# A fixed TensorE order for the mixer, MLP and routing of a Mamba2 and mixture-of-experts layer

## The chip, the cores and the metric

The kernel runs on one core of one Trainium2 chip. The metric is the device time of one execution in microseconds (us). The core has five engines that run side by side[...]: TensorE (PE; its weight loads are the row PEld), VectorE (DVE), ScalarE (ACT), GpSimd (POOL) and SyncE (SP), which here only issues DMAs. TensorE writes to PSUM[...]; the other engines read the results from there.

## The reference, cut to what matters

Input: 2048 tokens of width 512, float32. `A` is a layer of its own with an inner residual; the matrices are all float32.

```python
x = x + A(layernorm(x))                  # A: mixer, then MLP
x = x + E(layernorm(x))                  # E: experts

def A(u):
    h = u + mamba2(rmsnorm(u))
    h2 = rmsnorm(h)
    return h + (silu(h2 @ gate_w) * (h2 @ up_w)) @ down_w       # 512 -> 2048 -> 512

def mamba2(v):
    z, xb, B, C, dt = split(v @ in_proj_w)    # 1024, 256, 256, 1024, 16 columns
    xb, B, C = silu(causal_conv4(xb, B, C))
    dt = softplus(dt + dt_bias); dA = dt * -exp(A_log)          # 16 heads of 64
    # chunks of 128 tokens; L[q, s] = exp(cum[q] - cum[s]) for s <= q, cum = cumsum(dA)
    y = (C @ B.T * L) @ (xb * dt) + exp(cum) * (C @ state)
    state = state * exp(cum[-1]) + (B * exp(cum[-1] - cum)).T @ (xb * dt)
    y = rmsnorm((y + D * xb) * silu(z)) @ out_proj_w
    return y

def E(v):
    p = softmax(v @ Wr)                       # 8 experts, the 2 best, weights made to sum to 1
    return sum(w_e * (silu(v @ Wg[e]) * (v @ Wu[e])) @ Wd[e] for e in top2(p))  # 512 -> 352 -> 512
```

## The kernel before

**Tiles.** A chunk is 128 tokens (`P`), a token block two chunks (`TB` = 256, index `b`, 8 of them), an MLP block two token blocks (`FB` = 512, index `fb`, 4 of them).

**The mixer.** `prepare(b)` normalizes a block, transposes it into `hT` (L186), makes the step sizes dt and dA with some 20 small VectorE operations, and their sums `pc` (L246), `pn` and `psum`. The rows of sums go to HBM, and `spread` reads them back spread over partitions as `cum` and `ec`; GpSimd masks `cum` (L282). `project` makes one of six column pairs `pm` of the convolved part (16 matmuls, L301), ScalarE copies it to `pre` (L311), VectorE does the four taps (L318, L320), ScalarE the SiLU (L326). GpSimd keeps the three tokens that the next block needs in `halo`. `gate` makes the four pairs `pz` of silu(z). `chunk` is the core: transposes `ptx`, scores `psc` (L363), decays on ScalarE (L369), their product with the scores on VectorE (`cum`, L371, eight instructions for each half of the heads), `py` from the old state (L384) and from this chunk (L390), the new state `pst` (L397, L413), skip and gate (`yd` L403, `zs` L406), squares (L422 to L425, the sums on GpSimd), output projection `po` (L430), sum of squares `pms` (L432), its root `ry` (L142), the residual `h`, and a transposition of the normalized `h2` (L448) for the MLP.

**The MLP.** `feed_forward(fb)` runs 16 steps c over 128 columns of the hidden width each. The gate and up products of a step are made as a two by two block product with seven block multiplications instead of eight (`product`, L644: two matmuls of 256 columns each). Sums of the weights are made by GpSimd in the first pass (`load_early`, `load_late`), written to HBM on ScalarE's DMA queue and read in the later passes; sums of the activations come from `sums`. Two PSUM banks carry a step: `px` (tag x1) is written and read five times one after the other, `py` (tag x2) twice. Its readers are ScalarE copies (L665, L667, L675) and VectorE (L671, L679, L680, L685). `mlp_down` adds the previous two steps' contribution to the output for 128 tokens: two matmuls of 512 columns into `pd` (L629) and one VectorE addition into `r` (L630).

**Routing and experts.** `route(fb, rows)` normalizes the finished rows, transposes them (`xT`, copied by ScalarE, L188), makes the logits (L542), picks the two best with small VectorE operations, counts places, and builds lists of tokens with one-hot products `pls` (L606). `table` turns counts and lists into at most 39 tiles of 128 tokens. `tiles` then gathers each tile by an indirect DMA (L865), multiplies it with its expert's weights (L884, L896, L905), and adds it to the output by an indirect DMA (L911). The first eight tiles use the lists of the first three MLP blocks alone.

**What sets the order.** The stages are Python generators that are stepped against each other, and this is the source's order:

```python
for _ in mamba(b):          # one piece per yield of a chunk: three or four in each
    if feed:
        next(feed)          # one MLP step of the block before
    if tail:
        next(tail, None)    # one piece of the routing of the block before that
```

That order isn't the engines'. The Tile framework's planner gives each engine its own order by planned costs and due times, so that it may bring a matmul group forward or put it back. Instructions of one engine then run in the order given.

**PSUM.** Eight banks: `ps_x` two (`px`, `py`), `ps_mm` three under one tag (`pd`, `po`, `pm`, `pz`, and all transposes and small products), `ps_sg` two (`psc`), `ps_y` one (`py` of the chunk).

**The opening.** SP issues the loads of x, `params`, `w_dt`, two pairs of `w_in` (`wi`), then `w_o` (2 MB), then the router's weights. GpSimd scales `w_o` in eight instructions before it comes to the halo copies of the first block. `prepare(0)` runs to its end, `spread` follows, and then the six projections of block 0.

Of the kernel before, what the change touches and what calls it, by code (L numbers as in the profile page):

```python
# [49 lines left out]
def mamba_mlp_moe(ctx, tc, x, w_in, w_out, w_gu, w_down, par, wr, wg, wu, wd, out):  # L50
# [47 lines left out]
    nc.sync.dma_start(out=w_o, in_=w_out.rearrange("(t p) n -> p t n", p=P))  # L98
# [64 lines left out]
    ps_mm = psa_stack.enter_context(tc.tile_pool(name="ps_mm", bufs=3, space=PSUM))  # L163
# [3 lines left out]
    use = {"g": (ps_x, "x1"), "u": (ps_x, "x2"), "d": (ps_mm, "mm"), "tr": (ps_mm, "mm")}  # L167
# [24 lines left out]
    def prepare(b):  # L192

        scales(b)
        hT = wa.tile([P, NK, TB], F32, name=f"hT{b}", tag="hT")
        for j in range(NCH):
            t = b * NCH + j
            hn = wa.tile([P, D], F32, name=f"hn{t}", tag="tok", bufs=3)
            nc.vector.tensor_scalar(
                hn, res[t], mv[:, t, 0:1], rboth[:, t : t + 1], ALU.subtract, ALU.mult  # L200
            )
            transposed(hn, hT[:, :, j * P : (j + 1) * P], params[:, C_L1 : C_L1 + NK])
# [6 lines left out]
        pdt = ps_mm.tile([P, NCH, NH], F32, name=f"pdt{b}", tag="mm")  # L209
# [35 lines left out]
        pc = ps_mm.tile([P, P], F32, name=f"pc{b}", tag="mm")  # L245
# [5 lines left out]
        nc.sync.dma_start(out=rows_d.rearrange("a n q -> n a q"), in_=rows)  # L251

        pn = ps_mm.tile([P, NCH, NH], F32, name=f"pn{b}", tag="mm")
# [7 lines left out]
        psum = ps_mm.tile([P, 2, NCH, NH], F32, name=f"psum{b}", tag="mm")  # L261
# [32 lines left out]

    def projected(b, pair, pm, hT):
        w = ahead.pop(0)
        if b < NB - 1 or pair < 8:
            ahead.append(load_w_in((pair + 2) % 10))
        for m in range(2):
            for k in range(NK):  # L300
                nc.tensor.matmul(  # L301
                    pm[:, m, :], w[:, k, m * P : (m + 1) * P], hT[:, k, :], start=(k == 0), stop=(k == NK - 1)
                )

    def project(b, pair, hT, xb, cs):

        pm = ps_mm.tile([P, 2, TB], F32, name=f"pm{b}_{pair}", tag="mm")
        projected(b, pair, pm, hT)
# [19 lines left out]
    def gate(b, pair, hT, zs):  # L328

        pm = ps_mm.tile([P, 2, TB], F32, name=f"pz{b}_{pair}", tag="mm")  # L330
        projected(b, 6 + pair, pm, hT)
        nc.scalar.activation(zs[:, 2 * pair : 2 * pair + 2, :], pm, AF.Silu)
# [7 lines left out]

    def chunk(b, j, dt, ncum, dtdec, cd, cum, ec, xb, cs, zs):
        t = b * NCH + j
        tok = slice(j * P, (j + 1) * P)
        halves = [slice(half * HD, (half + 1) * HD) for half in range(2)]
        sdt = sdiag[t % 2]
        y = zs[:, :, tok]


        pt = ps_mm.tile([P, 4, P], F32, name=f"ptx{t}", tag="mm")
        for m in range(4):  # L350
            nc.tensor.transpose(pt[:, m, :], xb[:, m, tok], ident)
        xbt = wa.tile([P, 2, 4, HD], F32, name=f"xbt{t}", tag="xbt")
        nc.scalar.copy(xbt.rearrange("p a g d -> p (a g d)"), pt.rearrange("p a q -> p (a q)"))

        for gp in range(2):
# [18 lines left out]
            if gp == 0 and t < NT - 1:  # L374
# [5 lines left out]
                )  # L380
            py = ps_y.tile([P, 4, P], F32, name=f"py{t}_{gp}", tag="y")
# [6 lines left out]
            yield  # L388
            for half in range(2):
# [4 lines left out]
            if gp == 0 and t < NT - 1:  # L394
                pst = ps_mm.tile([P, 2, 4, HD], F32, name=f"pst{t}", tag="mm")
# [23 lines left out]


# [10 lines left out]
        pms = ps_mm.tile([P, 1], F32, name=f"pms{t}", tag="mm")  # L431
# [8 lines left out]
        nc.scalar.dma_start(out=resd[t], in_=res[t])  # L440
        yield
# [12 lines left out]

    for m in range(8):
        nc.gpsimd.tensor_scalar_mul(w_o[:, m, :], w_o[:, m, :], params[:, C_NW + m : C_NW + m + 1])
# [10 lines left out]
    def load_early(fb, c):  # L467

        w = pmlp.tile([P, 4, KH, FC], F32, name="mg", tag="mg", bufs=3)
        if fb == 0:  # L470
            nc.sync.dma_start(out=w[:, 0:2], in_=w_gu[c, :, 0])
            nc.sync.dma_start(out=w[:, 3], in_=w_gu[c, :, 1, 0])
        else:
            nc.sync.dma_start(out=w[:, 0:3], in_=early_d[c])
        return w

    def load_late(fb, c, w):

        v = pmlp.tile([P, 4, KH, FC], F32, name="ms", tag="mg", bufs=3)
        if fb == 0:  # L480
            nc.sync.dma_start(out=v[:, 3], in_=w_gu[c, :, 1, 1])
            nc.gpsimd.tensor_tensor(w[:, 2], w[:, 3], v[:, 3], ALU.add)
# [40 lines left out]
    def route(fb, rows):  # L523
# [6 lines left out]
        for j in range(NJ):  # L530
# [7 lines left out]
            xT = mid([NK, P], f"xT{t}")  # L538
            transposed(xn, xT)
            pl = bank("tr", [NE], f"pl{t}")  # L540
# [3 lines left out]
            if j % 2:  # L544
                yield
# [15 lines left out]
        yield  # L561
# [14 lines left out]
        nc.vector.tensor_tensor(before, prior[:, NJ - 1, :], both[:, NJ - 1, :], ALU.add)  # L576
        pr = bank("tr", [NJ, NE], f"pr{fb}")
        nc.tensor.matmul(pr, tri, both, start=True, stop=False)
        nc.tensor.matmul(pr, ones, prior, start=False, stop=True)

        yield
        pls = bank("tr", [2, P], f"pls{fb}")
        for n in range(2):

            at, hi, lo = small("at", NJ), small("hi", NJ), small("lo", NJ)
            nc.vector.tensor_tensor(tmp, chosen[n], pr, ALU.mult)
# [9 lines left out]
            nc.vector.tensor_tensor(ohl, bc(lo, 2, P), bc(count, 1, NJ), ALU.is_equal)  # L596
            for pair in range(NJ // 2):
# [7 lines left out]
                for j in range(2):  # L605
                    nc.tensor.matmul(  # L606
                        pls, ohl[:, 2 * pair + j, :], v[:, j],
                        start=(n == 0 and pair == 0 and j == 0), stop=(n == 1 and pair == NJ // 2 - 1 and j == 1),
                    )
            yield  # L610
        nc.vector.tensor_tensor(lists, lists, pls, ALU.add)
# [13 lines left out]
    def mlp_down(fb, rows, j, pair):  # L625

        pd = bank("d", [D], f"pd{fb}_{j}")
        for m, (a, d) in enumerate(pair):
            nc.tensor.matmul(pd, a[:, j * P : (j + 1) * P], d, start=(m == 0), stop=(m == 1))  # L629
        nc.vector.tensor_tensor(rows[j], rows[j], pd, ALU.add)  # L630

    def feed_forward(fb):
# [7 lines left out]
        held, pair = [], None  # L640
# [6 lines left out]

        for c in range(NFC):
            early, late_ = mlp_w
            more = fb < NFB - 1 or c < NFC - 1  # L650
            to = (fb, c + 1) if c < NFC - 1 else (fb + 1, 0)
            if more:
                coming = load_early(*to)
            if c == 1:
                for j in range(NJ):
                    rows.append(wk.tile([P, D], F32, name=f"r{fb}_{j}", tag="row", bufs=5))
                    nc.sync.dma_start(out=rows[j], in_=resd[fb * NJ + j])
            a = wk.tile([P, 2, FH], F32, name=f"a{fb}_{c}", tag="a", bufs=4)
            part = wk.tile([P, FH], F32, name=f"part{fb}_{c}", tag="part", bufs=1)
            up = wk.tile([P, FH], F32, name=f"up{fb}_{c}", tag="up", bufs=1)  # L660
            x1 = bank("g", [FH], f"px{fb}_{c}")
            x2 = bank("u", [FH], f"py{fb}_{c}")

            product(x1, early[:, 1], b21)
            nc.scalar.copy(a[:, 0], x1)  # L665
            product(x2, early[:, 2], t1)
            nc.scalar.copy(up, x2)  # L667
            if more:
                mlp_w = coming, load_late(*to, coming)
# [3 lines left out]
            product(x2, late_[:, 2], b22, False)  # L673
            product(x1, late_[:, 0], t2, False)
            nc.scalar.copy(part, x1)  # L675
            if pair:
                mlp_down(fb, rows, 2 * (c % 2), pair)
            product(x1, late_[:, 1], t3, False)
            nc.vector.tensor_tensor(a[:, 1], part, x2, ALU.add)  # L679
            nc.vector.tensor_tensor(up, up, x1, ALU.add)  # L680
            nc.scalar.activation(a[:, 1], a[:, 1], AF.Silu)
            if pair:
                mlp_down(fb, rows, 2 * (c % 2) + 1, pair)
            product(x1, late_[:, 3], t4, False)
            nc.vector.tensor_tensor(a[:, 0], a[:, 0], x1, ALU.mult)  # L685
            nc.gpsimd.tensor_tensor(a[:, 1], a[:, 1], up, ALU.mult)  # L686
            newest = a.rearrange("p h q -> p (h q)")
            held.append(newest)
            if c % 2:
                pair = [(h, load_down(n)) for h, n in zip(held, (c - 1, c))]  # L690
                held = []
            yield
        for j in range(NJ):
            mlp_down(fb, rows, j, pair)
# [5 lines left out]
    def finish(steps):  # L700
        while True:
            try:
                next(steps)
            except StopIteration as end:
                return end.value

    ready = finish(prepare(0))
    near = [spread(0, j, ready[-1]) for j in range(NCH)]

    xc = channels(0)  # L710
    for pair in range(6):
        project(0, pair, ready[0], *xc)

    def mamba(b):
# [12 lines left out]
        for j in range(NCH):  # L727
            for _ in chunk(b, j, dt, ncum, dtdec, cd, *near[j], xb, cs, zs):
                if more and n == 0:
                    next_hT = next(coming)  # L730
                elif more and n < 3:
# [3 lines left out]
                if n < 2:  # L735
                    for pair in (2 * n, 2 * n + 1):
                        gate(b, pair, hT, zs)
                elif more:
                    project(b + 1, n - 2, next_hT, *xc)
                n += 1  # L740
                yield
# [6 lines left out]
    tail = None  # L748
    for fb in range(NFB):
        feed = feed_forward(fb - 1) if fb else None  # L750
        for b in range(fb * BPF, (fb + 1) * BPF):
            for _ in mamba(b):
                if feed:
                    next(feed)
                if tail:
# [27 lines left out]
    def table(n, name, used=None):  # L783
# [34 lines left out]
        nc.vector.tensor_copy(exp_i, exp_f)  # L818
        plt = bank("tr", [2, P], f"plt{name}")
# [3 lines left out]
        nc.vector.tensor_copy(lists_t, plt)  # L823
        pi = bank("tr", [2, n], f"pi{name}")
# [22 lines left out]
    first = None  # L847
    for c in range(NFC):
        next(feed)
        if first is None and next(tail, 0) == 0:  # L850
            first = table(NS1, "1")
        if c in CALL:
            e = CALL.index(c)
            nc.gpsimd.tensor_copy(ew[:, e, 0:EW:EI], newest[:, 0 : len(range(0, EW, EI))])
            load_expert(e)

# [13 lines left out]
    def front(s, xg):  # L870
        xT = mid([NK, P], f"xgT{s}")
# [20 lines left out]
    def turned(s, h):  # L892
# [4 lines left out]
        hT = mid([len(ET), P], f"ehT{s}")  # L897
# [30 lines left out]
    def tiles():  # L928


        fetch(0)
        last = None
# [16 lines left out]
    work = tiles()  # L949
# [72 lines left out]
```

## The time and the profile before

| what | value |
|---|---|
| time before, median of 3 runs | 1641.17 us (1638.57 to 1647.05) |
| profiled execution: its own time, its span | 1641.24 us, 1639.5 us |
| mean granted TensorE clock | 0.988 of full speed |
| PE busy | 1560.9 us, 95% of the span, 6283 matmuls |
| PEld (weight loads, beside PE) | 1056.3 us, 64% |
| DVE busy | 780.5 us, 48% |
| ACT busy | 714.9 us, 44% |
| POOL busy | 401.5 us, 24% |
| DMA | 216.57 MB, mean 132 GB/s |

The span runs from the first to the last instruction of the profiled execution. Busy time of an engine leaves out register, branch, semaphore and DMA-issuing instructions; PE's time includes only modelled ends of pipelined matmuls. A row with "<-" names what ended a wait: `PE px L644 <- DVE a L671` means that a matmul of line 644 into `px` waited for VectorE's instruction of line 671. All times in the text are us unless marked ns. Where the stages lie: opening to about 54 us, mixer of the first 512 tokens (token blocks 0 and 1) alone to 224, mixer of token blocks 2 to 7 beside the MLP of the first three MLP blocks to 1110, the last MLP block alone to 1286, its end beside the first tiles to 1370, experts to the end.

### The profile page before, as it was taken

Reading aid. Unit: us, or ns where it says so; the run is one execution under the profiler, and the core shown is the slowest. Engines: PE = TensorE matmul, PEld = TensorE weight load, DVE = VectorE, ACT = ScalarE, POOL = GpSimd, SP = SyncE. Lnnn points to the kernel's source line nnn. Section 1 sums busy time; section 2 is a strip of 40 time slices with the busy share of each in tenths; the row PEclk is TensorE's granted clock in tenths of the full one; section 3 lists DMA queues with packets and bytes.
Section 4 is the critical chain, followed back from the end, with each engine's and each line's share of the span. In section 5 each row is a group of like instructions: output and inputs, shape, how many; then the busy total and the mean of one; then the engine's idle time right before and its main releaser. Section 6 shows DMA issues by size and latency. Waiting matters only on the chain. (4 is left out here: it accounts for less than half of the span.)

```text
span 1639.5 us, 19005 instructions
## 1 busy us (share of the span) xinstructions
PE 1560.9 (95%) x6283; PEld 1056.3 (64%) x6283; DVE 780.5 (48%) x2011; ACT 714.9 (44%) x1316; POOL 401.5 (24%) x486
## 2 busy tenths in 40 slices
PE   4998989999999999999999999999999989999997
PEld 4666666657666766766677667666776545666663
DVE  4776763654555557455465653334533343222221
ACT  2987857444653565455636454523211211111110
POOL 5132333342333112110221121111010113333331
PEclk9999989999999999999999999999999999999999
DMA  8353534544543554343445432326886223333332
GB/s 276 114 160 96 150 106 142 165 155 126 178 164 116 176 165 148 96 141 108 130 154 181 129 112 81 112 84 236 275 263 202 66 51 59 68 67 65 66 66 35
DMA packets 122975, 216.57 MB, mean 132 GB/s; under 512 B 11200, under 2 KB 64960, under 8 KB 122880
## 3 DMA queue, kind: packets, MB, share of 16 engines
q1 hardware_dynamic: 100608, 163.98, 32.3%
q0 software_dynamic: 8736, 20.45, 7.2%
q10 hardware_dynamic: 13536, 30.94, 5.1%
q8 instruction: 52, 0.85, 0.2%
q14 instruction: 43, 0.35, 0.1%
HBM read 173.91 MB, written 41.42 MB: 131 GB/s over the span
## 5 line engine op out<-in xcount | busy, mean ns | idle before, releaser
L629 PE MATMUL pd<-md,a 128*128 128x512 f32 x512 | 244.2, 592 | 0.0
L301 PE MATMUL pm<-hT,wi 128*128 128x256 f32 x768 | 185.0, 395 | 4.9 <-DMA wi<-in_w_in 4.8
L301 PEld LDWEIGHTS pm<-hT,wi 128*128 128x128 f32 x768 | 148.1, 197 | 35.8 <-ACT pre L311 5.2
L686 POOL TENSOR_TENSOR a<-a,up 128x256 f32<-128x256 f32 x64 | 46.8, 732 | 396.0 <-DVE up L680 281.2
L644 PE MATMUL px<-ts,ms 128*128 128x256 f32 x512 | 134.9, 386 | 7.8 <-DVE a L671 7.6
L644 PE MATMUL px<-h2T,mg 128*128 128x256 f32 x512 | 135.0, 385 | 4.7 <-ACT a L665 4.6
L320 DVE SCALAR_TENSOR_TENSOR ca<-pre,params,ca 128x256 f32<-128x256 f32 x288 | 136.4, 538 | 0.1
L629 PEld LDWEIGHTS pd<-md,a 128*128 128x128 f32 x512 | 97.5, 191 | 58.9 <-issue 47.6
L644 PEld LDWEIGHTS px<-ts,ms 128*128 128x128 f32 x512 | 91.5, 191 | 65.0 <-DVE a L671 21.5
L630 DVE TENSOR_TENSOR r<-r,pd 128x512 f32<-128x512 f32 x128 | 87.8, 686 | 86.9 <-PE pd L629 85.7
L884 PE MATMUL epg<-ew,xgT 128*128 x312 | 119.2, 464 | 0.8 <-ACT xgT L188 0.6
L884 PE MATMUL epu<-ew,xgT 128*128 x312 | 117.9, 459 | 0.0
L301 PE MATMUL pz<-hT,wi 128*128 128x256 f32 x512 | 115.9, 385 | 0.0
L644 PEld LDWEIGHTS px<-h2T,mg 128*128 128x128 f32 x512 | 94.9, 190 | 29.4 <-ACT a L665 8.8
L430 PE MATMUL po<-w_o,zs 128*128 128x512 f32 x256 | 113.8, 593 | 0.0
L905 PE MATMUL epd<-ew,ehT 128*128 (+1 forms) x234 | 108.1, 597 | 0.5 <-DVE ehT L898 0.5
L301 PEld LDWEIGHTS pz<-hT,wi 128*128 128x128 f32 x512 | 97.6, 193 | 13.6 <-ACT cs L326 0.8
L369 ACT ACT_TABLE_LOAD x76 | 97.5, 1283 | 1.2
L369 ACT ACTIVATE cum<-cum,ncum 128x128 f32<-128x128 f32 x256 | 86.6, 393 | 23.2 <-POOL cum L282 22.4
L865 POOL DMA_INDIRECT xg<-xnd,idx x39 | 38.7, 992 | 195.7 <-PE pt L186 185.8
L430 PEld LDWEIGHTS po<-w_o,zs 128*128 128x128 f32 x256 | 48.5, 190 | 52.6 <-issue 51.4
L671 DVE TENSOR_TENSOR a<-a,px 128x256 f32<-128x256 f32 x64 | 26.6, 415 | 114.2 <-PE px L644 108.8
(242 smaller groups left out, 2425.8 us busy)
## 6 DMA issues: line engine op xcount, KB each, us to landing
wi<-in_w_in SPq DMA_DIRECT2D x80, 512.0 KB, 3.8
ms<-late SPq DMA_DIRECT2D x48, 512.0 KB, 3.6
mg<-early SPq DMA_DIRECT2D x48, 384.0 KB, 3.2
md<-in_w_down SPq DMA_DIRECT2D x64, 256.0 KB, 2.8
cum<-rowsd SPq DMA_DIRECT2D x32, 512.0 KB, 4.7
late<-ms ACTq DMA_DIRECT2D x16, 512.0 KB, 3.6
ec<-rowsd SPq DMA_DIRECT2D x60, 128.0 KB, 3.9
xnd<-xn ACTq DMA_DIRECT2D x28, 256.0 KB, 3.6
```

What stands on the lines that cost most here:

```text
L301: nc.tensor.matmul(pm[:, m, :], w[:, k, m * P : (m + 1) * P], hT[:, k, :], start=(k == 0), stop=(k == NK - 1))
L320: nc.vector.scalar_tensor_tensor(ca, pre[:, m, k : k + TB], cw[:, k : k + 1], ca, ALU.mult, ALU.add)
L369: nc.scalar.activation(lt[:, half, i], lt[:, half, i], AF.Exp, bias=ncum[:, j, h : h + 1])
L430: nc.tensor.matmul(po, y[:, m, :], w_o[:, m, :], start=(m == 0), stop=(m == 7))
L629: nc.tensor.matmul(pd, a[:, j * P : (j + 1) * P], d, start=(m == 0), stop=(m == 1))
L630: nc.vector.tensor_tensor(rows[j], rows[j], pd, ALU.add)
L644: nc.tensor.matmul(ps, w[:, k], m[:, k], start=(first and k == 0), stop=(k == KH - 1), skip_group_check=True)
L671: nc.vector.tensor_tensor(a[:, 0], a[:, 0], x1, ALU.add)
L686: nc.gpsimd.tensor_tensor(a[:, 1], a[:, 1], up, ALU.mult)
L865: nc.gpsimd.indirect_dma_start(out=xg, out_offset=None, in_=src, in_offset=bass.IndirectOffsetOnAxis(ap=idx[:, n : n + 1], axis=0))
L884: nc.tensor.matmul(ps, xT[:, k, :], w[:, lo : lo + EI], start=(k == 0), stop=(k == NK - 1))
L905: nc.tensor.matmul(pd, hT[:n, m, :], w[:n, NG + m * D : NG + (m + 1) * D], start=(m == 0), stop=(m == len(ET) - 1))
```

## The change

- **Order.** From `fb == 1` (the third token block; MLP work runs beside the mixer from here) to the end, TensorE runs in the source's order: `tc.manual_schedule(engines={PE})`. The other engines are still ordered by the planner, and TensorE is too before that point.
- **MLP in finer pieces.** `feed_forward` yields four times a step instead of once. The fifth product of a step (`fifth`: early third quarter times t1) is made one step ahead, and the fourth one with t4 (`fourth`) at the start of the next step. `mlp_down` is a generator that can be stopped between its two matmuls; half of one down product's matmuls is put on each side of a step's first product. The tile `part` is dropped, `up` has two buffers.
- **Mixer in finer pieces.** `chunk` yields more often and `mamba` has five slots for each of its four turns, with a projection stopped at half. The transposes `ptx` are made a chunk ahead (`turned_x`). `prepare` yields between its transposes and between its small products.
- **PSUM.** `ps_mm` keeps two banks (`pd`, `po`, `pm`, `pz`, logits `pl`); a new `ps_tr` has one for transposes and small products (`pt`, `pdt`, `pc`, `pn`, `psum`, `ptx`, `pst`, `pms`, `pr`, `pls`).
- **Opening.** The first block's projections are issued ahead of and between the pieces of its step sizes. The load of `w_o` and its eight scalings come after the third projection.
- **First MLP pass.** `load_early` also loads the fourth quarter of the weights and makes its sum there; `load_late` loads that quarter again.
- **Routing.** One transposition per piece, logits a piece later, counts copied out of PSUM, lists added for each of the two choices. In the mixer stages, every fourth piece steps the routing. `table` yields twice. The experts' `xgT` and `ehT` move to the buffers of tag `a`.

The diff, cut to its core (line numbers above 640 in the new file are some 12 to 60 higher than in the old one):

```diff
-    nc.sync.dma_start(out=w_o, in_=w_out.rearrange("(t p) n -> p t n", p=P))
...
-    ps_mm = psa_stack.enter_context(tc.tile_pool(name="ps_mm", bufs=3, space=PSUM))
+    ps_tr = psa_stack.enter_context(tc.tile_pool(name="ps_tr", bufs=1, space=PSUM))
+    ps_mm = psa_stack.enter_context(tc.tile_pool(name="ps_mm", bufs=2, space=PSUM))
...
+        for j in range(NCH):
+            yield
+            transposed(hns[j], hT[:, :, j * P : (j + 1) * P], params[:, C_L1 : C_L1 + NK])
...
+    def turned_x(t, xb):
...
+        yield
+        if t < NT - 1:
+            xbts[t + 1] = turned_x(t + 1, xb if j == 0 else xc[0])
...
-    for m in range(8):
-        nc.gpsimd.tensor_scalar_mul(w_o[:, m, :], w_o[:, m, :], params[:, C_NW + m : C_NW + m + 1])
...
             nc.sync.dma_start(out=w[:, 0:2], in_=w_gu[c, :, 0])
+            nc.sync.dma_start(out=w[:, 2], in_=w_gu[c, :, 1, 1])
             nc.sync.dma_start(out=w[:, 3], in_=w_gu[c, :, 1, 0])
+            nc.gpsimd.tensor_tensor(w[:, 2], w[:, 3], w[:, 2], ALU.add)
...
+        def fifth(c, early):
+            x2 = bank("u", [FH], f"py{fb}_{c}")
+            product(x2, early[:, 2], t1)
+            up = wk.tile([P, FH], F32, name=f"up{fb}_{c}", tag="up", bufs=2)
+            nc.scalar.copy(up, x2)
+            made[c] = x2, up
+
+        def fourth(a, x1, up, late):
+            product(x1, late[:, 3], t4, False)
+            nc.vector.tensor_tensor(a[:, 0], a[:, 0], x1, ALU.mult)      # L698
+            nc.gpsimd.tensor_tensor(a[:, 1], a[:, 1], up, ALU.mult)      # L699
...
+            if last:
+                fourth(*last)
...
+            down = mlp_down(fb, rows, 2 * (c % 2), pair) if pair else iter(())
+            next(down, None)
...
             product(x1, early[:, 1], b21)
             nc.scalar.copy(a[:, 0], x1)
+            next(down, None)
+            yield
+            if c == 0:
+                fifth(c, early)
             product(x1, early[:, 0], b11)
             nc.vector.tensor_tensor(a[:, 0], a[:, 0], x1, ALU.add)
             nc.scalar.activation(a[:, 0], a[:, 0], AF.Silu)
+            x2, up = made.pop(c)
+            product(x2, late[:, 2], b22, False)
...
+            yield
+            product(x1, late[:, 0], t2, False)
+            nc.scalar.copy(a[:, 1], x1)
             if pair:
+                finish(mlp_down(fb, rows, 2 * (c % 2) + 1, pair))
+            nc.vector.tensor_tensor(a[:, 1], a[:, 1], x2, ALU.add)
+            nc.scalar.activation(a[:, 1], a[:, 1], AF.Silu)
+            yield
+            product(x1, late[:, 1], t3, False)
             nc.vector.tensor_tensor(up, up, x1, ALU.add)                 # L743
...
+                if c < NFC - 1:
+                    fifth(c + 1, early)
...
+    coming = prepare(0)
+    for _ in range(3):
+        hT = next(coming)
+    next(coming)
...
+        finish(project(0, pair, hT, *xc))
+        if pair < 2:
+            next(coming)
+        elif pair == 2:
+            ready = finish(coming)
+            near = [spread(0, j, ready[-1]) for j in range(NCH)]
+            nc.sync.dma_start(out=w_o, in_=w_out.rearrange("(t p) n -> p t n", p=P))
+            for m in range(8):
+                nc.gpsimd.tensor_scalar_mul(w_o[:, m, :], w_o[:, m, :], params[:, C_NW + m : C_NW + m + 1])
+    xbts[0] = turned_x(0, xc[0])
...
+        if fb == 1:
+            in_order.enter_context(tc.manual_schedule(engines={mybir.EngineType.PE}))
...
+            for piece in mamba(b):
...
+                n += 1
                 if feed:
                     next(feed)
+                if tail and n % 4 == 3:
                     next(tail, None)
```

## The prediction

> **What bounds the kernel now.** I read the busy table first, then the busy time by stage, then TensorE's waits, then both timelines around one hand-over. In the busy table TensorE has 95% of the span:
>
> ```profile
> PE 1560.9 (95%) x6283; PEld 1056.3 (64%) x6283; DVE 780.5 (48%) x2011; ACT 714.9 (44%) x1316; POOL 401.5 (24%) x486
> ```
>
> So a new order can win at most the 78.6 us in which TensorE stands still, and the time it spends at a lowered clock. The table by stage (start and end in us, width, then busy time and instructions of PE, PEld, DVE, ACT, POOL, clock, DMA share, GB/s) says where those are: opening, first 512 tokens, three stages of mixer with MLP, MLP alone, junction to the experts, experts.
>
> ```profile
> 0.00:54.00 54.00, 32.58 (x126) 27.61 (x127) 27.68 (x81) 22.33 (x41) 25.30 (x45) 0.94 0.75 245
> 54.00:224.00 170.00, 152.10 (x665) 104.47 (x664) 119.75 (x316) 143.13 (x236) 48.68 (x65) 0.95 0.40 122
> 224.00:560.00 336.00, 328.22 (x1352) 226.69 (x1351) 179.83 (x447) 168.62 (x312) 110.71 (x144) 1.00 0.48 152
> 560.00:900.00 340.00, 336.80 (x1451) 237.81 (x1450) 188.71 (x505) 187.36 (x340) 64.89 (x86) 1.00 0.45 142
> 900.00:1110.00 210.00, 207.14 (x818) 139.51 (x817) 101.11 (x261) 96.09 (x174) 34.09 (x43) 1.00 0.33 103
> 1110.00:1286.00 176.00, 172.01 (x671) 121.52 (x670) 76.30 (x202) 38.65 (x90) 19.15 (x29) 0.99 0.69 228
> 1286.00:1370.00 84.00, 73.56 (x293) 45.06 (x292) 31.75 (x106) 17.70 (x32) 17.82 (x15) 0.98 0.27 61
> 1370.00:1640.00 270.00, 258.46 (x918) 153.67 (x916) 55.31 (x98) 40.99 (x95) 80.90 (x62) 0.99 0.36 62
> ```
>
> Idle TensorE, width less busy: 21.4, 17.9, 7.8, 3.2, 2.9, 4.0, 10.4, 11.5 us. The stretch that gets a fixed order (224 to 1110 and on) holds little: 13.9 us. The waits of the opening, and the two that make up most of the junction:
>
> ```profile
> PE pt L186 <- DVE hn L199: 9.9, 1, 9.9
> PE pc L246 <- DVE dA L243: 6.3, 1, 6.3
> PE pm L301 <- DMA wi<-in_w_in: 4.8, 1, 4.8
> ...
> PE pls L606 <- DVE v L604: 5.3, 4, 1.4
> PE pl L542 <- ACT xT L188: 2.6, 3, 1.0
> ```
>
> [...]below, a wait of 2.33 us, and the next 16 records take 6.71 us where the same group takes 3.70 at 126.07. [...]at 655.22 TensorE waited 0.91 us for L671, queued behind a convolution block although its operand had been ready for 2 us. [...]before 2+3+2+1, after 2+1+2+2+1, so all eight stay in use. [...]the trace's mean is 1283.
>
> ```profile
> 206.75 0.59 PE L432 MATMUL pms<-ones,sq 128*128 128x1 f32 x2 [2.33 <-POOL sq L425]
> 207.20 6.71 PE L301 MATMUL pm<-hT,wi 128*128 128x256 f32 x16
> ```
>
> **The change part by part.** TensorE's work is the same; only where it waits moves. Times are against the profiled execution, 1641.24 us (span 1639.5 and 1.7 around it), which is the median, 1641.17, in effect.
>
> *Opening.* The projections no longer wait for the step sizes (6.3 us), and w_o's 2 MB load stands behind the third wi. That doesn't win 11 us, because ScalarE waits too: its first pre copy (34.10) needs a halo copy that POOL ran at 33.64, after eight w_o scalings (12.4 us) and four weight sums. In the new program two halo copies go ahead of the scalings, the third behind them and five sums (0.73 each). With w_o landing 1.6 us later (512 KB at the opening's 330 GB/s; it landed at 18.3), POOL comes to the third at 19.9+12.4+3.7 = 36.0. Before, six pairs took 34.8 to 60.1, 4.2 each; now four are left, 36+17 = 53, and 60-53 = 7. I take **-6**; bounds -11 (both waits gone) and 0 (ScalarE, 5.9 of 6 us busy from 42 on, gives it back).
>
> *First 512 tokens (mixer alone).* ScalarE is 143 of 170 us busy, and its table loads there stay about equal. The transposition of h2 (L448) stands one projection later: of its waits, 1.4, 4.0, 0.95 and 2.7 us, I take 3 us off. But eight early MLP matmuls that the planner had put into this block's gaps (137.83 to 216.5) no longer come before the fixed stretch: 1.7 us go back. And the second chunk's pms loses cover: its sums of squares start behind the last py, and before some 10.5 us of products stood between, which already fell short by 2.1 and 2.3 us (125.83, 206.75); now there are three half projections (1.3), po (6.9) and a transposition group (0.45), 8.7: 1.8 more, twice, 3.6. **+2**; bounds -6 and +6.
>
> *Fixed order, mixer with MLP.* Every MLP step c hands bank px over five times, each to a VectorE or ScalarE read. Four have a mixer piece or two down products between; the fifth, from `fourth` (L698) to the next step's first product, has one 0.86 us matmul. Alone L698 needs 0.17+0.42+0.1 = 0.7 and is covered. In the built program it isn't alone: at c = 0, 4, 8 and 12 of all three passes VectorE has yd x4, state, zs and the eight cum products right ahead of it. (L698, L699 and L743 are lines of the new file, the others of the old.) Their time is in the trace; first VectorE's timeline, then TensorE's at the same place (start, duration, the idle time before in brackets):
>
> ```profile
> 778.10 1.12 DVE L403 SCALAR_TENSOR_TENSOR yd<-xb,params,py 128x128 f32<-128x128 f32 x4 [0.60 <-PE py L390]
> 779.14 0.68 DVE L413 TENSOR_TENSOR state<-state,pst 128x512 f32<-128x512 f32 x1
> 779.74 0.68 DVE L406 TENSOR_TENSOR zs<-yd,zs 128x512 f32<-128x512 f32 x1
> 780.34 2.14 DVE L371 SCALAR_TENSOR_TENSOR cum<-cum,dt,psc 128x128 f32<-128x128 f32 x8
> ```
>
> ```profile
> 777.88 1.03 PE L397 MATMUL pst<-xd,xbt 128*64 128x256 f32 x8
> 778.84 1.13 PE L363 MATMUL psc<-cs,xb 64*128 64x512 f32 x4
> ```
>
> From py's end (777.9) VectorE needs to 782.5, with L698 to 782.9: 5.0 us. TensorE has pst 0.96, psc 1.06, the fourth product 0.86, half a down product 0.86 = 3.74. Stall **1.25 us** for a block's first chunk. For its second a convolution block (2 x 0.3 and 6 x 0.41 at 785.78, up to 4.1 at 800) and the state scaling on POOL, behind L699, come before: about 11.0 against 9.1, **1.95**. Six blocks: 19. Where cum of the first half stands ahead of L698 (c = 3, 7, 11): 0.65 and 0.2 a block, 5. L743 behind a convolution block: 0.25 x 5 = 1. Two routings in the middle put 3.2 us of one-hot products ahead of L743: 3.2 each = 6.5. Steps c = 0 and 1 have no down products as cover: 0.8 x 3 = 2.5. In the first MLP pass ScalarE issues the weight sums' stores, and waits for POOL with the px copies queued behind: 0.4 x 16 = 6. A lowered clock after some stalls: 3. Sum 43, against 17.8 us idle from 246 to 1265 that I let go whole, since four of five hand-overs are better covered than before. The MLP-only part is in that figure: L698's 0.7 against 0.86 just holds. **+25**; bounds -18 and +55 (each of the 12 long stalls halving the clock for 3 us, the routings' doubled).
>
> *Costing nothing.* ScalarE's loads fall from 224 to 193 in the built programs: 31 x 1.28 = 40 us of an engine that is half idle in these stages; no gain while it isn't the bound, and if it were, a few us less stall. The first pass loads a third quarter twice: 16 x 128 KB, 16 more issues on SP of 0.45 us; DMA share 0.48 and buffers asked for a step ahead hide it. One bank for transposes: between two users stand 3.4 us of products or more, a copy takes 0.58 to 0.69. Two banks for po, pm, pd: the closest, po to pm, has 3.85 us, and its release (sqrt 0.26, reciprocal 0.16, L698, h 0.75) 2.6. Without that cover each is 0.5 us per chunk, 6 in all; it is in the upper bound.
>
> *Junction and experts.* xT's copies get half a tile as cover: the logits' waits (2.6) and half the one-hot waits go. New: logits to counts with only one down product (2.6 us) ahead of some 4 us of small VectorE work, 1.5; the second one-hot group 2; 0.5 for the first. 10.4 becomes about 4: **-6**; bounds -8 and +3. The experts are back to back before and after: 0.
>
> Sum: -6 + 2 + 25 - 6 = +15, **1656 us**.
>
> **Rivals.** *The hand-overs are hidden (faster).* If VectorE comes to cum earlier than I think, since the exponentials are a chunk ahead, L698 is never late: -6 + 2 - 18 - 6, 1613; with the first 512 tokens at their -6, 1605. For it: VectorE is busy half the time. Against: the cum block stands ahead of L698 in every pass. It decides if VectorE's chain is under 3.7 us from py's end. *The clock falls (much slower).* Stalls of 2 us at a regular distance drop it as at 206.75; 12 x 3 us more gives 1692, about 1690. For it: that line. Against: at 125.83 a wait of 2.12 us left the next group at 3.70. *Even.* Stalls of 25 us in the middle instead of 43: 1638. That TensorE's order isn't what the source says is excluded: the built program has it.
>
> **How the numbers follow.** My case and the worse one: 0.53. Even, within 0.5% (8 us, about what a measurement can tell): 0.20. Hidden: 0.27. The range takes the hidden rival's low end and the clock rival's high end, 1605 to 1690; the likeliest case alone is 1640 to 1674.
>
> **What would show it.** Right: TensorE waits "px <- DVE a" from L698 as the top wait after the opening, some 21 times, 1 to 2 us each, at psc; idle 224 to 1110 at 30 us or more; the wi wait gone, pm from about 15; ScalarE's loads 193. Wrong: that stretch idle under 15 us, or L698 with no TensorE wait behind it; then the total is under 1632.

## The result, and the profile after

The changed kernel takes 1705.14 us (median of 4, 1699.6 to 1707.15) against 1640.34 before: a ratio of 1.0382, with a 95% interval of 1.0344 to 1.042. It is slower by 65 us, four times what I had forecast, and above the range.

The profiled execution has a span of 1697.8 us, 58.3 more than before. Its busy table (busy time, share of the span, instructions):

```profile
PE 1570.2 (92%) x6283; PEld 1056.4 (62%) x6283; DVE 758.8 (45%) x2019; ACT 677.1 (40%) x1285; POOL 390.8 (23%) x486
```

TensorE has the same 6283 matmuls. It stands still for 127.6 us instead of 78.6, and its busy time grows by 9.3. No other engine has become the bound: VectorE, ScalarE and GpSimd are all less busy than before. So the question is where TensorE waits. The busy time by stage, cut where the first chunk is transposed (ptx), and where the sums of the first and of the last MLP block begin; columns as in the table of before:

```profile
0.00:51.20 51.20, 33.20 (x127) 27.60 (x128) 23.70 (x77) 18.48 (x31) 24.90 (x45) 0.93 0.78 253
51.20:223.00 171.80, 155.20 (x668) 103.72 (x665) 125.68 (x321) 143.32 (x243) 49.09 (x67) 0.97 0.42 127
223.00:1175.60 952.60, 885.90 (x3633) 607.41 (x3634) 452.16 (x1229) 417.73 (x796) 200.04 (x271) 0.99 0.41 130
```

The mixer with MLP before, cut in the same places:

```profile
223.00:1111.30 888.30, 874.17 (x3626) 605.58 (x3627) 471.71 (x1216) 453.05 (x828) 211.04 (x273) 1.00 0.43 136
```

All four parts, before and after (us; idle TensorE of the mixer with MLP in the last column):

| | opening | first 512 tokens | mixer with MLP | last MLP block to end | idle in mixer with MLP |
|---|---|---|---|---|---|
| before | 54.3 | 168.7 | 888.3 | 528.2 | 14.1 |
| after | 51.2 | 171.8 | 952.6 | 522.2 | 66.7 |
| difference | -3.1 | +3.1 | +64.3 | -6.0 | +52.6 |
| predicted | -6 | +2 | +25 | -6 | |

The loss is in the mixer with MLP. The cuts are made in time and don't divide TensorE's work at quite the same matmul: the last part holds 1874 matmul records before and 1859 after. TensorE stands still in it for 25.5 us before and 26.3 after, so its -6.0 us are not fewer waits.

The two largest waits of TensorE in the mixer with MLP before (total, times, longest), and then the waits after:

```profile
PE px L644 <- DVE a L671: 7.6, 12, 1.2
PE px L644 <- ACT a L665: 4.6, 6, 1.3
```


```profile
PE py L684 <- DVE a L739: 34.4, 22, 2.8
PE px L684 <- DVE a L698: 19.5, 16, 1.8
PE px L684 <- DVE up L743: 6.2, 5, 1.9
PE py L684 <- DVE ts L656: 2.7, 1, 2.7
PE px L684 <- ACT a L736: 2.1, 4, 0.8
PE px L684 <- ACT a L722: 2.0, 2, 1.1
```

The wait for L698, which I had put at the centre, is there. But a larger one stands above it, and it isn't in the prediction: bank `py` waits for L739, 22 times, and each time a whole convolution block stands ahead of L739 on VectorE. One such place, first TensorE's timeline, then VectorE's:

```profile
787.75 1.88 PE L666 MATMUL pd<-md,a 128*128 128x512 f32 x4
789.47 1.03 PE L684 MATMUL px<-h2T,ms 128*128 128x256 f32 x4
792.89 1.26 PE L684 MATMUL py<-ts,mg 128*128 128x256 f32 x4 [2.39 <-DVE a L739]
793.95 1.06 PE L186 MATMUL pt<-ident,h 128*128 128x128 f32 x4
794.94 2.08 PE L383 MATMUL psc<-cs,xb 64*128 64x512 f32 x4
```

```profile
788.92 0.61 DVE L331 TENSOR_SCALAR ca<-pre,params 128x256 f32<-128x256 f32 x2 [0.74 <-ACT pre L324]
789.45 2.46 DVE L333 SCALAR_TENSOR_TENSOR ca<-pre,params,ca 128x256 f32<-128x256 f32 x6
791.82 0.68 DVE L669 TENSOR_TENSOR r<-r,pd 128x512 f32<-128x512 f32 x1
792.42 0.41 DVE L739 TENSOR_TENSOR a<-a,py 128x256 f32<-128x256 f32 x1
```

`fifth(c + 1)` writes bank `py` (the second line for `py` in `feed_forward`, a step ahead). The bank comes free when L739 has read it. On VectorE L739 stands behind a whole convolution block (0.61 + 2.46 us) and an addition into `r` (0.68). TensorE has 3.4 us of products from the end of the projection (787.05), VectorE needs 5.8 us from there. It stands for 2.39 us, although the transposition `pt` and the scores `psc`, next in line, need nothing from `py`. And then comes a second cost: `psc` takes 2.08 us here, 1.13 elsewhere. The granted clock is 0.50 from 793.76 to 797.17.

### The profile page after: what moved, and what is told of

The parts are those of the page before. It is cut to its first block, busy times and chain, and to the rows that moved or that the text cites. A ratio compares the mean times of both kernels' runs of the same rounds, so it can differ in the third digit from the quotient of the medians.

```text
span 1697.8 us, 18859 instructions
## 1 busy us (share of the span) xinstructions
PE 1570.2 (92%) x6283; PEld 1056.4 (62%) x6283; DVE 758.8 (45%) x2019; ACT 677.1 (40%) x1285; POOL 390.8 (23%) x486
## 5 line engine op out<-in xcount | busy, mean ns | idle before, releaser
L666 PE MATMUL pd<-md,a 128*128 128x512 f32 x512 | 249.6, 596 | 0.0
L312 PE MATMUL pm<-hT,wi 128*128 128x256 f32 x768 | 191.7, 398 | 0.0
L684 PE MATMUL px<-h2T,mg 128*128 128x256 f32 x512 | 135.6, 387 | 22.5 <-DVE a L698 19.5
L699 POOL TENSOR_TENSOR a<-a,up 128x256 f32<-128x256 f32 x64 | 46.5, 726 | 399.1 <-DVE up L743 303.6
L333 DVE SCALAR_TENSOR_TENSOR ca<-pre,params,ca 128x256 f32<-128x256 f32 x288 | 129.9, 516 | 0.2
L684 PE MATMUL py<-ts,mg 128*128 128x256 f32 x256 | 73.2, 411 | 42.4 <-DVE a L739 34.4
L684 PEld LDWEIGHTS py<-ts,mg 128*128 128x128 f32 x256 | 48.1, 198 | 60.0 <-issue 24.7
L970 POOL DMA_INDIRECT xg<-xnd,idx x39 | 38.6, 991 | 181.3 <-PE pt L186 174.6
```

Of the source, the lines that this page charges most:

```text
L312: nc.tensor.matmul(pm[:, m, :], w[:, k, m * P : (m + 1) * P], hT[:, k, :], start=(k == 0), stop=(k == NK - 1))
L333: nc.vector.scalar_tensor_tensor(ca, pre[:, m, k : k + TB], cw[:, k : k + 1], ca, ALU.mult, ALU.add)
L684: nc.tensor.matmul(ps, w[:, k], m[:, k], start=(first and k == 0), stop=(k == KH - 1), skip_group_check=True)
L970: nc.gpsimd.indirect_dma_start(out=xg, out_offset=None, in_=src, in_offset=bass.IndirectOffsetOnAxis(ap=idx[:, n : n + 1], axis=0))
```

## The experiments

The theory from here on: the loss is TensorE standing, in a fixed order, at bank hand-overs for which VectorE is late, above all at L739 and L698, plus the clock that goes with some of the stops (0.50 at the one above). The rivals are the new pieces themselves, the split of the banks, and that removing one late hand-over only shows the next. Medians are against 1640 to 1641 us for the kernel before in each group of runs.

**1. The planner orders TensorE again.**

```diff
         if fb == 1:
-            in_order.enter_context(tc.manual_schedule(engines={mybir.EngineType.PE}))
+            pass
```

> The changed kernel, but TensorE's order is left to the planner again; pieces, banks, opening and routing stay as changed. Theory (the fixed order makes TensorE stand at bank hand-overs that VectorE is late for): the planner can put other work there, so most of the 52.6 us of added idle time between 223 and 1175 us goes: 1640 to 1660 us. Rival (the new pieces, the fifth product a step ahead or the split of the banks cost it, whoever orders TensorE): 1690 us or more.

Measured: 1613.86 us, a ratio to before of 0.9829 (0.9791 to 0.9866). Taking out one line wins 91 us, 26 us beyond the theory's range: all the rest of the change, for which I had -10 us (opening, first 512 tokens, junction), makes the kernel 27 us faster than before. TensorE's waits in the mixer with MLP are all these:

```profile
PE px L684 <- DVE up L743: 2.2, 2, 1.1
PE py L684 <- DVE a L739: 0.6, 2, 0.5
PE pd L666 <- DVE r L669: 0.6, 1, 0.6
```

The same place of the same step in this run, TensorE and then VectorE:

```profile
744.22 1.03 PE L684 MATMUL px<-h2T,ms 128*128 128x256 f32 x4
745.08 0.60 PE L186 MATMUL pt<-ident,h 128*128 128x128 f32 x4
745.61 1.13 PE L383 MATMUL psc<-cs,xb 64*128 64x512 f32 x4
746.67 0.49 PE L406 MATMUL py<-ec,sdiag 128*128 128x128 f32 x2
747.63 1.13 PE L684 MATMUL py<-ts,mg 128*128 128x256 f32 x4 [0.47 <-DVE a L739]
```

```profile
743.66 0.62 DVE L331 TENSOR_SCALAR ca<-pre,params 128x256 f32<-128x256 f32 x2 [0.74 <-ACT pre L324]
744.19 2.46 DVE L333 SCALAR_TENSOR_TENSOR ca<-pre,params,ca 128x256 f32<-128x256 f32 x6
746.56 0.68 DVE L669 TENSOR_TENSOR r<-r,pd 128x512 f32<-128x512 f32 x1
747.16 0.42 DVE L739 TENSOR_TENSOR a<-a,py 128x256 f32<-128x256 f32 x1
```

VectorE does the same four groups in the same order and is just as late. TensorE has moved `pt`, `psc` and the start of the chunk's `py` ahead of the fifth product, and waits 0.47 us instead of 2.39. Its idle time in this stage is 4.7 us (873.8 less 869.1):

```profile
225.60:1099.40 873.80, 869.13 (x3611) 602.54 (x3609) 450.96 (x1217) 417.72 (x796) 201.36 (x271) 1.00 0.44 140
```

**2. The convolution's taps a piece later,** TensorE in the fixed order, instruction for instruction: from 223 us on both traces list the same 5490 matmuls in the same sequence.

```diff
         nc.gpsimd.tensor_copy(hl, pre[:, :, TB : TB + 3])
+        yield
         for m in range(2):
...
                     next_hT = next(coming)
+                next(halves, None)
                 yield
```

> The changed kernel with TensorE's order untouched; the taps of a convolution are only issued one piece later, so that L739 (second half of a, which frees bank py) has two or three of a block's eight operations ahead of it on VectorE instead of all eight and an addition into r. Theory: the 22 waits of 34.4 us for L739 shrink below 8 us, and with them a few us of lowered clock: 27 to 40 us less than the changed kernel, 1665 to 1678. Rival (VectorE's work is only pushed behind L739 and makes the next hand-over late instead, L743 or L698): less than 10 us gained, with px <- L743 or L698 up by what py <- L739 loses.

Measured: 1656.08 us (ratio 1.0081, 1.0056 to 1.0106), 49 us less than the changed kernel, more than the theory's 27 to 40. L739 now has mostly two or three of the eight operations ahead of it (six at two steps of the first MLP pass). Lines are one higher in this kernel: L740 is L739, L699 is L698, L744 is L743. Its waits over the whole run, and its mixer with MLP:

```profile
PE px L685 <- DVE a L699: 21.8, 20, 1.8
PE px L685 <- DVE up L744: 6.7, 5, 2.4
PE py L685 <- DVE a L740: 3.0, 7, 0.6
```

```profile
223.80:1133.30 909.50, 874.29 (x3633) 605.85 (x3634) 453.41 (x1228) 429.17 (x804) 202.54 (x271) 0.99 0.43 136
```

The wait went from 34.4 to 3.0, and the other two did not take it over (L698 went from 19.5 to 21.8 over the whole run, L743 from 9.2 to 6.7). The stage became 43 us shorter: 31.5 of idle time (66.7 to 35.2) and 11.6 of busy time (885.9 to 874.3), with 3633 matmul records in both. Some 8 of the 11.6 us are the clock's. This is an estimate from the two traces: in this stage TensorE is busy at a granted clock of 0.50 for 26.4 us in the changed kernel and for 10.2 us here, and half of the difference is lost time (at that clock four matmuls of 256 columns took 2.07 us at 848.97 in the changed kernel, and 1.03 at full clock at 1221.96). The other 3.5 us are not explained. The two profiled executions are 38.6 us apart, the medians 49.

**3. The fifth product in its own step.**

```diff
-            if c == 0:
-                fifth(c, early)
+            fifth(c, early)
...
-                if c < NFC - 1:
-                    fifth(c + 1, early)
-                else:
+                if c == NFC - 1:
                     mlp_w = coming
```

> The changed kernel, but the fifth product of each MLP step is made in its own step, between its first and second product, as step 0 does already, not a step ahead; VectorE's order stays. Theory (what is tight is the place of this hand-over: py is wanted 0.86 us after its reader could start): the L739 waits go, and only a part comes back at L743, whose cover loses 0.86 us: 20 to 35 us less than the changed kernel, 1670 to 1685. Rival (VectorE is late at this place whichever bank is asked for): the waits return as px <- L743 and the gain is under 10 us.

Measured: 1673.87 us (1.0188, 1.0147 to 1.0228), 31 us less. The wait for L739 is gone, but part of it is back at the instruction behind it (L742 is L743):

```profile
PE px L684 <- DVE a L698: 24.6, 20, 2.0
PE px L684 <- DVE up L742: 22.2, 26, 2.8
```

L743's wait grew by 13 us (9.2 to 22.2 over the whole run), L698's by 5. So VectorE is late at this place whichever bank is asked for; the place of the fifth product decides how much of it TensorE feels. The gain is the theory's, but 18 of the 34.4 us came back, so the rival's mechanism holds in part.

**4. The cum products a piece later.** TensorE's order in the fixed stretch stays; `xd` moves with the first half's products.

```diff
-            for half, i, h in turns:
-                nc.vector.scalar_tensor_tensor(
-                    lt[:, half, i], lt[:, half, i], dt[:, j, h : h + 1], psc[:, half, i], ALU.mult, ALU.mult
-                )
-            if gp == 0 and t < NT - 1:
...
+            def decayed():
+                for half, i, h in turns:
+                    nc.vector.scalar_tensor_tensor(
+                        lt[:, half, i], lt[:, half, i], dt[:, j, h : h + 1], psc[:, half, i], ALU.mult, ALU.mult
+                    )
+
             if gp:
                 yield
+                decayed()
...
             yield
             if gp == 0:
+                decayed()
+                if t < NT - 1:
...
                 yield
```

> The changed kernel with TensorE's order in the mixer with MLP untouched; the eight products of decays and scores (cum, L391) are issued a piece later, so that at steps 0, 4, 8, 12 L698 has three of them ahead of it instead of eight, and at steps 3, 7, 11 six. Theory: 12 waits of 0.98 to 1.84 us for L698 (14 us together) go, the others shrink by a third: 12 to 18 us less than the changed kernel, 1687 to 1693. Rival (py of the chunk, which needs cum, becomes late instead): under 5 us gained, with new waits py <- cum.

Measured: 1678.9 us (1.0234, 1.0191 to 1.0277), 26 us less; the theory had 12 to 18. The wait for L698 (L702 here) falls from 19.5 to 5.4 us, the one for L739 (L743 here) stays:

```profile
PE py L688 <- DVE a L743: 34.0, 22, 2.6
...
PE px L688 <- DVE a L702: 5.4, 7, 1.4
```

No wait of `py` for cum has come. Again the gain is larger than the wait that went.

**5. Both shifts together, fixed order.** The edits of 2 and 4.

> The changed kernel with TensorE in the source's order and both shifts on VectorE: the convolution's taps and the cum products a piece later. Theory (the two hand-overs are separate, and each wait costs TensorE its own time): the gains add up, 49 + 26 = 75 us, 1630 us, and between 223 us and the last MLP block TensorE stands for 25 us or less. Rival (taking one away only lets the next late hand-over show): 1645 us or more, that is under 11 us on top of the convolution's shift alone.

Measured: 1634.23 us (0.9956, 0.9943 to 0.997), 71 us less than the changed kernel; 49 and 26 are 75. The two add up, and TensorE in the source's order is now slightly faster than the kernel before. The idle time between 221 and 1107.7 us is 18.7 us.

**6. The fixed order only from the last MLP block on.** The line of experiment 1 is entered where `tail = routed(tail)` stands.

> The changed kernel with TensorE in the source's order only from the last MLP block on (routing, tables, experts); the mixer stages are left to the planner. Theory (nearly all of the order's cost is in the mixer with MLP, where VectorE's convolutions and cum products stand ahead of the bank readers): the stretch to 1100 us is as in the run with the planner, and the tail costs what it cost with the fixed order, 522.2 against 512.7 us in the profiles: 1614 + 9 = 1623 us. Rival (the order costs where single waits are long, weights and routing in the tail): 1650 us or more.

Measured: 1631.7 us (0.9938, 0.9919 to 0.9957), 18 us more than with the planner throughout, and not the 9 that I expected. In the profiles the last stage takes 529.6 us with the fixed order there, 512.7 with the planner. So of the order's 91 us some 18 lie in the tail, which leaves about 73 for the mixer with MLP. The rival's place is wrong, my size too: I had compared stretches that don't hold the same work. The changed kernel's 522.2 us hold 1859 matmul records, the 512.7 us with the planner 1871.

**7. Planner, with the old PSUM pool** (three banks under one tag).

> As the first run (planner orders TensorE), with PSUM as it was before: three banks under one tag in place of two and one. Theory (prediction: between two users of a bank lies enough other work, so the split costs and gains nothing): 1606 to 1622 us, no difference from 1614. Rival (the split is what makes the rest of the change faster, transposes no longer queue for a bank with the down products): 1630 us or more.

Measured: 1615.55 us (0.9854, 0.9809 to 0.99), 1.7 us from the run with the split: no difference. In the fixed order this wasn't tried.

**8. Planner, with the old opening.**

> As the first run (planner orders TensorE), with the opening as it was before: step sizes ahead of all projections of the first block, w_o's load and scalings at their old places. Theory: the opening is worth about what the profiles show at the transposition ptx, 54.3 against 51.3 us, so 1615 to 1620 us. Rival (it is worth the two waits that it takes away, 11 us): 1622 us or more.

Measured: 1615.36 us (0.9849, 0.9812 to 0.9885), 1.5 us from the run with the new opening. Nothing that the runs can tell; the rival's 11 us are not there.

**9. Planner, with both shifts on VectorE.**

> As the first run (planner orders TensorE), with the two shifts on VectorE of the fifth run (convolution taps and cum products a piece later). Theory: where TensorE has other work at a late hand-over VectorE's order hardly matters, so what was worth 71 us with the fixed order is worth under 8 us here: 1606 to 1622 us. Rival (VectorE's lateness costs in itself): 1600 us or less.

Measured: 1606.28 us (0.9789, 0.9761 to 0.9817). The two edits that were worth 71 us in the fixed order are worth 7.6 here, just inside the bound. With the fixed order the same program takes 1634.23 us (experiment 5): 28 us of the order's cost stay even when VectorE's bulk work is out of the way.

**10. Planner, with the fifth product in its own step.**

> As the first run (planner orders TensorE), with the fifth product in its own step. Theory: the product a step ahead is a piece that the planner can place freely, its place in the source costs nothing here: 1610 to 1620 us, no difference. Rival (having the fifth product a step ahead is what wins the 14 us between 225 and 1100 us against the kernel before): 1624 us or more.

Measured: 1607.33 us (0.9811, 0.9776 to 0.9846; single runs 1601.9 to 1614.0), 6.5 us less than with the product a step ahead. The theory said no difference. The runs spread too far to call it a gain, but the rival is out: the early fifth product is not what wins time.

**11. Planner, old routing function,** one pool of banks.

> As the run with the planner and one pool of banks (1615.6 us), with the old routing function: two transpositions and their logits in one piece, counts left in PSUM, one-hot products of both choices into one bank. Theory: the finer routing is worth the waits for logits and one-hot operands that are gone from the junction's profile, some 8 us: 1620 to 1627 us. Rival (the junction's gain is from the stepping of table and tiles, not from the routing): within 4 us of 1615.6.

Measured: 1620.93 us (0.9878, 0.9837 to 0.9919), 5.4 more than run 7. It is on the theory's side, but the intervals overlap.

**12. The candidate: planner, both shifts, fifth product in its own step.**

> The candidate: planner orders TensorE, both shifts on VectorE, and the fifth product in its own step; all else as changed. Theory (with TensorE idle for some 50 us of 1610 only, and most of it in the opening and the first 512 tokens, which these edits don't touch): the two gains of 7 us overlap, 1598 to 1607 us. Rival (they add up): 1592 to 1598.

Measured: 1602.92 us (0.9777, 0.9746 to 0.9807). It lies where the theory had it and beats both kernels: 37 us below the one before. The largest waits that are left are in the opening and in the first 512 tokens:

```profile
PE pt L186 <- DVE hn L200: 9.1, 1, 9.1
PE pms L464 <- POOL sq L457: 8.0, 2, 4.2
PE pn L258 <- ACT rows L252: 6.5, 1, 6.5
```

## Why the prediction was wrong

- **The step that failed is the first sentence of the fixed order:** "Every MLP step c hands bank px over five times". It counts one bank of the two. `py` is handed over too, from L739 to the fifth product, and the change had just moved that product from the next step to a place one product behind. That wait took 34.4 us; I had nothing for it. A convolution block of 3.1 us was in my text; with the addition into `r` (0.68 in the trace) it stands against 3.4 us of products. I had even seen a convolution block ahead of L743, one instruction later, and priced 0.25 us for it. Experiment 2 shows the cause: with the block moved behind L739 the wait falls to 3.0 us and the kernel by 49.
- **The clock was mis-sized.** I put 3 us. TensorE's busy time in this stage grew by 11.7 (874.2 to 885.9), and it was busy at half clock for 26.4 us against 3.7 before, by the estimate of experiment 2 some 11 us lost. The rival in which the clock falls had the right effect on the wrong stops: it tied it to the 12 stops at L698, and none of the seven drops goes with one of these. Five go with a stop at L739, one with L743, one with `ts`.
- **The sum.** Between +25 and the +64.3 measured lie 39 us: 34.4 of the missing hand-over, 8.7 of busy time (11.7 less 3), 3.7 because less idle time was there to lose (14.1 and not 17.8), and -7.7 because the other stops came to 32.3 us (66.7 less 34.4) and not 40.
- **The terms that I did count came near in sum, in part by luck.** L698: 19 + 5 + 2.5 expected, 19.5 measured. The twelve stops at c = 0, 4, 8, 12 came as said, with 14.7 us instead of 21.5; those expected at c = 3, 7, 11 (5 us) came twice, 2.0 us, just behind a routing; two more, 2.8 us, stand behind the routings' own small operations. L743: 7.5 expected, 6.2 measured, but 3.5 of it behind convolution blocks, where I had 1, and 2.1 behind the routings' one-hot products, where I had 6.5. ScalarE's copies of px: 6 expected in the first MLP pass, 4.1 measured, of which 2.1 are in that pass.
- **The opening** came out at -3.1 in the profiles instead of -6, and experiment 8 finds nothing that can be told. The wait for the step sizes went; `pn` now waits 6.5 us for ScalarE's rows (L252). The trace shows ScalarE itself starting late: it stood 9.8 us for a weight sum of GpSimd (L499) before it came to the table of the first SiLU at 33.5 us.
- **First 512 tokens:** +3.1 against +2, but by other terms: TensorE's idle time fell by 1.0 us and its busy time grew by 4.1. **Junction and experts:** -6.0 as predicted, by luck: the idle time that I meant to win didn't fall (25.5 to 26.3), the part holds 15 matmul records and 6.8 us of busy time less. With the planner it is 15.5 us shorter than before (512.7 against 528.2), with 16.0 us of idle time, and experiment 6 shows the fixed order costing 17 to 18 there when it stands alone.
- **What I held to cost nothing** shows no cost: the split of the banks makes no difference with the planner (experiment 7), and in the fixed order no wait of the mixer with MLP over 0.5 us is for one of these banks. The table loads of ScalarE (`ACT_TABLE_LOAD`, 1283 ns each in both traces) are 193, 31 fewer, and ScalarE's busy time is down 37.8 us; what that alone is worth wasn't tried.
- **The rivals.** The hidden hand-overs fell with 66.7 us of idle time. The even case fell too. Of the signs that I had named, more than 30 us of idle time came; L698 as the top wait didn't. What none of them had is that the rest of the change is worth 27 us when TensorE isn't bound to the source's order.

What stays open is how these 27 us are made up. In the profiles 24.9 of 27.4 us are idle time of TensorE: 6.0 before the mixer with MLP, 9.4 in it, 9.5 behind it. Of the parts that were tried alone, the banks (1.7), the opening (1.5) and the routing (5.4) are not told from the noise, and the early fifth product points the wrong way.

## What to carry to other kernels

Before an engine is put into a fixed order, list every hand-over of every bank and buffer of that engine, with the reader that frees it, and add up what stands ahead of that reader on its own engine. Here the block and the addition ahead of L739 decided (0.61 + 2.46 + 0.68 us at the place shown), not L739's own 0.41 us. If the order is to be fixed, fix the other side as well: two shifts of VectorE's bulk work behind the small bank readers won back 71 of 91 us here. A planner that may swap two independent matmul groups hid the same lateness here: 4.7 us of idle time in this stage, and not 66.7.

## What the runs showed of the hardware

In the traces of the two kernels the granted clock of TensorE is 1.00 or 0.50. In the mixer with MLP it is 0.50 at seven places of the changed kernel, each of them at a stop of TensorE of 1.94 to 2.79 us. The length of the stop alone doesn't tell where. Here are the same four matmuls of the changed kernel after no stop (clock 1.00), after one of 1.94 us (0.50), and in the last MLP block after one of 2.40 us (1.00):

```profile
433.48 1.03 PE L684 MATMUL px<-ts,ms 128*128 128x256 f32 x4
540.78 1.73 PE L684 MATMUL px<-ts,ms 128*128 128x256 f32 x4 [1.94 <-DVE up L743]
1225.38 1.13 PE L684 MATMUL px<-ts,ms 128*128 128x256 f32 x4 [2.40 <-DVE up L743]
```

The two waits of the kernel before that the prediction held against each other differ in the same way. At the 2.33 us before 206.75 the clock was 0.50, and the next 16 records took 6.71 us. At the 2.12 us before 125.83 it stayed at 1.00, and the same group took 3.70:

```profile
125.83 0.38 PE L432 MATMUL pms<-ones,sq 128*128 128x1 f32 x2 [2.12 <-POOL sq L425]
126.07 3.70 PE L301 MATMUL pm<-hT,wi 128*128 128x256 f32 x16
```

What decides between such stops, the traces don't show. Where the clock was 0.50, a stop cost more than its own time: the one of 2.39 us before 792.89 another 1.6 us (1.26 for 1.03, 1.06 for 0.60, 2.08 for 1.13). That is part of why experiment 2 won more than its waits, some 8 us by the estimate there. In experiment 4 TensorE's busy time in this stage fell as well (885.9 to 875.0 us, with 21 matmul records fewer); how much of that is the clock's was not shown.
